# Search thresholds one and two of the second attention computed on GpSimd, the third prepared there, and a normalization ordered behind them

## Chip, cores and metric

The kernel runs on one core of a Trainium2 chip. Its time is the device time of one launch in microseconds (us); the median of three runs is given. A core has a matrix engine (TensorE, PE in the profile, with weight loads shown apart as PEld), a vector engine (VectorE, DVE), an engine for activation functions (ScalarE, ACT), a fourth one for elementwise work (GpSimd, POOL) and a queue that issues DMAs (SP). Each runs its own instructions in order, and they wait for each other through semaphores.

## What is computed

A graph network of four layers over 3327 nodes with 256 features, each followed by a residual and a layer norm. Only the fourth layer is touched. It runs two steps of a "top-p" attention beside a plain diffusion with the adjacency matrix:

```python
def _top_p_attention(X, W1, W2, W3):
    q = X @ W1.T @ W2.T
    k = X @ W3.T
    logits = q @ k.T / TAU
    probs = jax.nn.softmax(logits, axis=-1)
    idx = jnp.argsort(-probs, axis=-1)
    sp = jnp.take_along_axis(probs, idx, axis=-1)
    cs = jnp.cumsum(sp, axis=-1)
    keep_sorted = cs - sp < TOP_P
    rows = jnp.arange(probs.shape[0])[:, None]
    mask = jnp.zeros(probs.shape, dtype=bool).at[rows, idx].set(keep_sorted)
    A = probs * mask
    return A / jnp.maximum(A.sum(-1, keepdims=True), 1e-12)
...
for n in range(STEPS):
    A = _top_p_attention(Xa, W1, W2, W3)
    Xf = R @ Xf
    Xa = A @ Xa
    Z = Z + Xf @ U1[n].T + Xa @ U2[n].T
h = X + Z
mu = h.mean(-1, keepdims=True)
var = jnp.mean((h - mu) ** 2, axis=-1, keepdims=True)
return (h - mu) / jnp.sqrt(var + LN_EPS) * ln_g + ln_b
```

TOP_P is 0.9 and STEPS is 2; the result is added to the layer's input and normalized once more. So each row of 3327 probabilities keeps its largest entries until they hold 0.9 of the mass. Nothing is sorted in the kernel: it looks for the smallest value that is kept, row by row.

## The kernel before

The nodes are padded to 3328 and cut into 26 tiles of 128 rows. The second attention is a pipeline over these tiles, with three tiles in flight (the loop at line 1423). For one tile these pieces run:

- `scores` (line 1032): TensorE multiplies queries and keys, ScalarE copies the logits from PSUM into the tile `e` (128 x 3328), in four pieces.
- `search_long` (line 1162): finds each row's cut, and is the function that changes. It is a generator; the loop calls it step by step between TensorE's pieces of work. Its passes over all of `e` run on ScalarE, each with a sum along the row: an exponential at half scale (line 1177, `root`), the exponential itself (1179, `total`), a Relu and a Sign against the first threshold `c1` (1192, 1194: mass and count above it), and the same against a second threshold `c2` (1224, 1226). Between the passes stand short runs of arithmetic on one number per row: `c1` from `root` and `total` (1182 to 1190), `c2` by a step from the first mass and count (1196 to 1212), and the bound `c3` by a secant through both (1228 to 1238). `c3` lies above the cut by a margin, so that the cut is among the largest entries below it: VectorE writes each half of `e` with everything above `c3` set to zero (1244), takes the eight largest of each 128 columns (1111), ranks the largest 48 (1122, 1124), finds the cut `v` by a running sum (1131 to 1134), drops surplus equal values (1274) and masks `e` (1282).
- `attended` (line 1088): TensorE transposes the masked `e` block by block (1095), ScalarE copies the transposed blocks into `wt` (copies of this stage are listed under line 1030, where the in-order copy is made), TensorE multiplies them with `G` (1099).
- `diffused` (line 1072): adjacency tiles are loaded by SP (`at`, 1064), TensorE multiplies them with `F` (1066), VectorE scales the sum into `xf` (1085); GpSimd prepares its addend `t` (1076, 1080), part of which SP reloads from memory (`s` from `sd`, 1079).
- `second` (line 1323): the result's rows: VectorE adds attention and diffusion (1326), statistics (88, 89); GpSimd takes the root of the variance (829, 830), normalizes (1334 to 1336), then statistics again, and ScalarE writes the normalized rows (1345), which waits for GpSimd's `nb` (1344).

The order on each engine is made by a scheduler from the program's order and priorities, except where it is fixed: `here(...)` keeps an instruction in program order (all of ScalarE's passes and copies of this stage are kept so, and TensorE's score matmuls), and `tc.issue_after(x)` lets instructions be issued only after `x`. Before the change `issue_after(bound[0].ins)` holds the `match_replace` at line 1274 behind the last instruction of `c2` (line 1212). A row whose cut turns out not to be resolved to a tolerance sends its tile through a slow repeat (`again`, line 1532) after the loop.

Of the kernel before, what the change touches and what calls it, by code (L numbers as in the profile page):

```python
# [9 lines left out]
F32 = mybir.dt.float32  # L10
# [3 lines left out]
ALU = mybir.AluOpType  # L14
# [4 lines left out]
P = 128  # L19
# [28 lines left out]
def gnn_kernel(ctx: ExitStack, tc: tile.TileContext, n: int, a: dict, out: bass.AP):  # L48
# [771 lines left out]
    with tc.tile_pool(name="l3", bufs=1) as pool, tc.tile_pool(name="l3d", bufs=1, space=DRAM) as dram:  # L820
# [184 lines left out]
        sd = dram.tile([nt, P, D], F32, name="sd")  # L1005
        u1, u2 = (load(pool, x) for x in ("U1", "U2"))
        g3, b3 = (load_row(pool, x) for x in ("ln3_g", "ln3_b"))
        factors = pool.tile([P, 4], F32, name="factors")
        for k, x in enumerate((-0.5, -1.0, 0.3, 1.5)):
            nc.vector.memset(factors[:, k:k + 1], x)  # L1010
        ones = pool.tile([P, 8 * max(RP0, RPT)], F32, name="ones")
        nc.vector.memset(ones, 1.0)
# [144 lines left out]
            yield  # L1157

        junks = [None]
        bound = [None]  # L1160

        def search_long(work, sm, e, total, v, kept, halves=False):

# [4 lines left out]
            def t(name):  # L1168
                return t1(sm, name)
# [6 lines left out]
            yield  # L1176
            here(nc.scalar.activation(junk, e, AF.Exp, bias=neg[:, 0:1], scale=0.5, accum_out=root))
            yield
            here(nc.scalar.activation(e, e, AF.Exp, bias=neg[:, 1:2], accum_out=total))
            yield  # L1180
            lim = t("lim")
            nc.gpsimd.tensor_scalar(lim, total, -TOP_P, None, op0=ALU.mult)
            c1 = t("c1")
            nc.vector.reciprocal(c1, root)
            nc.vector.tensor_mul(c1, c1, total)
            nc.vector.scalar_tensor_tensor(c1, c1, 0.301, c1, op0=ALU.mult, op1=ALU.mult)


            nc1, f1, sg, k1, m1 = t("nc1"), t("fs1"), t("sg"), t("k1"), t("m1")
            nc.vector.tensor_scalar_mul(nc1, c1, -1.0)  # L1190
            yield
            here(nc.scalar.activation(junk, e, AF.Relu, bias=nc1, accum_out=f1))
            yield
            here(nc.scalar.activation(junk, e, AF.Sign, bias=c1, scale=-1.0, accum_out=sg))
            yield
            nc.vector.tensor_scalar(k1, sg, -0.5, npad / 2, op0=ALU.mult, op1=ALU.add)
            nc.vector.scalar_tensor_tensor(m1, k1, c1, f1, op0=ALU.mult, op1=ALU.add)
            rc, na = t("rc"), t("na")
            nc.vector.reciprocal(rc, c1)
            nc.vector.tensor_scalar(na, m1, lim, rc, op0=ALU.add, op1=ALU.mult)  # L1200

            den, nu, p, q = t("den"), t("nu"), t("p"), t("q")
            nc.vector.tensor_scalar(den, k1, 0.5, UNDER, op0=ALU.mult, op1=ALU.add)
            nc.vector.reciprocal(den, den)
            nc.vector.tensor_scalar(nu, na, UNDER, den, op0=ALU.add, op1=ALU.mult)
            nc.vector.tensor_scalar(p, nu, 0.0, 1.0, op0=ALU.max, op1=ALU.add)
            nc.vector.tensor_sub(q, p, nu)
            nc.vector.reciprocal(q, q)
            c2 = t("c2")
            nc.vector.scalar_tensor_tensor(c2, p, c1, q, op0=ALU.mult, op1=ALU.mult)  # L1210
            nc2, f2, k2, m2 = t("nc2"), t("fs2"), t("k2"), t("m2")
            bound[0] = nc.vector.tensor_scalar_mul(nc2, c2, -1.0)

            big = t("big")
            nc.gpsimd.tensor_tensor(big, k1, na, op=ALU.subtract)
            nc.gpsimd.tensor_scalar(big, big, 32.0, HUGE, op0=ALU.is_lt, op1=ALU.mult)

            s, dm, ends, same = t("s"), t("dm"), t1(sm, "ends", 2), t("same")
            nc.gpsimd.tensor_tensor(s, c2, c1, op=ALU.subtract)
            nc.gpsimd.tensor_scalar(same, s, 0.0, None, op0=ALU.is_equal)  # L1220
            nc.gpsimd.tensor_tensor(s, s, same, op=ALU.add)
            nc.gpsimd.tensor_scalar(ends, factors[:, 2:], k1, 1.0, op0=ALU.mult, op1=ALU.max)
            yield
            here(nc.scalar.activation(junk, e, AF.Relu, bias=nc2, accum_out=f2))
            yield
            here(nc.scalar.activation(junk, e, AF.Sign, bias=c2, scale=-1.0, accum_out=sg))
            yield
            nc.vector.tensor_scalar(k2, sg, -0.5, npad / 2, op0=ALU.mult, op1=ALU.add)
            nc.vector.scalar_tensor_tensor(m2, k2, c2, f2, op0=ALU.mult, op1=ALU.add)
            nc.vector.reciprocal(s, s)  # L1230
            nc.vector.tensor_sub(dm, m1, m2)
            nc.vector.tensor_mul(s, s, dm)
            nc.vector.tensor_scalar(s, s, ends[:, 0:1], ends[:, 1:2], op0=ALU.max, op1=ALU.min)
            nc.vector.reciprocal(s, s)
            c3 = t("c3")
            nc.vector.scalar_tensor_tensor(c3, c2, UNDER, m2, op0=ALU.mult, op1=ALU.add)
            nc.vector.tensor_scalar(c3, c3, lim, s, op0=ALU.add, op1=ALU.mult)
            nc.vector.scalar_tensor_tensor(c3, c3, c2, big, op0=ALU.add, op1=ALU.max)
            rest, base = t("rest"), t("base")
            cand = candidates(work)  # L1240
            for h, r in enumerate((rest, base)):
# [28 lines left out]
            for i, c in enumerate((0, half)):  # L1270
                drop = drops[:, i, :]
                part = e[:, c:c + half]
                with tc.issue_after(bound[0].ins):
                    nc.vector.match_replace(part[:, ::-1], drop, part[:, ::-1], 0.0)
                if halves:
                    nc.vector.scalar_tensor_tensor(part, part, v, part, op0=ALU.is_ge, op1=ALU.mult,
                                                   accum_out=sums[:, i:i + 1])
# [45 lines left out]
        def second(work, psum, it, acc, f, xf):  # L1323

            h = work.tile([P, D], F32, name="h")
            nc.vector.scalar_tensor_tensor(h, acc, f, xf, op0=ALU.mult, op1=ALU.add)
            xb = work.tile([P, D], F32, name="t")
            nc.gpsimd.tensor_tensor(xb, X[:, it, :], b3, op=ALU.add)
            mv = small.tile([P, 2], F32, name="mv")
            stats(mv, h)  # L1330
            rs = small.tile([P, 1], F32, name="rs")
            power(rs, mv)
            yield
            nc.gpsimd.tensor_scalar(h, h, mv[:, 0:1], rs, op0=ALU.subtract, op1=ALU.mult)
            nc.gpsimd.tensor_tensor(h, h, g3, op=ALU.mult)
            nc.gpsimd.tensor_tensor(h, h, xb, op=ALU.add)
            yield
            mv = small.tile([P, 2], F32, name="mv")
            stats(mv, h, here)
            rs = small.tile([P, 1], F32, name="rs")  # L1340
            power(rs, mv)
            yield
            nb = small.tile([P, 1], F32, name="nb")
            nc.gpsimd.tensor_scalar(nb, mv[:, 0:1], rs, -1.0, op0=ALU.mult, op1=ALU.mult)
            here(nc.scalar.activation(h, h, AF.Identity, scale=rs, bias=nb))  # L1345
            m = min(P, n - it * P)
            nc.sync.dma_start(out[it * P:it * P + m, :], h[:m, :])
            yield
# [29 lines left out]
        with tc.tile_pool(name="l3w", bufs=2) as work, tc.tile_pool(name="l3s", bufs=4) as sm, \  # L1378
# [41 lines left out]
            with tc.tile_pool(name="l3q", bufs=3, space=PSUM) as psum:  # L1420
                es, searches, xfs = {}, {}, []
                result = iter(())
                for i in range(-2, nt + 1):
# [52 lines left out]
                    if 0 < i:  # L1476
                        f = normalizer(sm, kepts[1][:, i - 1:i], tots[1][:, i - 1:i])
                        result = second(work, psum, i - 1, next(values), f, xfs[i - 1])
                both(result)
                fl = unresolved(sm, psum, 1)  # L1480

            fi0 = pool.tile([1, nt + 1], I32, name="fi0")
# [140 lines left out]
```

## Time and profile before

| | |
|---|---|
| median of three runs | 3515.73 us (3509.28, 3515.73, 3515.77) |
| the profiled execution: its time | 3512.67 us |
| the profiled execution: its span | 3510.8 us |
| granted TensorE clock over the span | 0.965 |
| busy PE | 3228.0 us (92%) |
| busy DVE | 2374.3 us (68%) |
| busy ACT | 1737.1 us (49%) |
| busy POOL | 932.2 us (27%) |
| first and last mask of the second attention (line 1282) start at | 2710.3 and 3449.0 us |

The shares are means over four layers with different limits; what a change in the second attention is worth has to be read in the stretch from about 2650 us to the end. There the stretches from one tile's first transpose to the next show how full each engine is, and the idle time ahead of TensorE's transposes shows who is late. Times in the rows are microseconds from the span's start; a bracket at the end of a row is the idle time of the engine ahead of it and what ended it. In rows of groups the first figure behind the bar is the sum of busy time in us, the second the mean of one instruction in ns.

### The profile page before, as it was taken

The page shows a single profiled execution, that of the slowest core. Times are in us where ns is not written, and L with a number is a line of the kernel's source. Part 1 is how long each engine was busy: PE and PEld are TensorE (multiplying, and loading weights), DVE is VectorE, ACT ScalarE, POOL GpSimd, SP SyncE. Part 2 cuts the span into 40 slices and gives each one's busy share as a digit, 9 for nine tenths or more (in the row PEclk, how much of TensorE's full clock was granted, in tenths as well). Part 3 has the DMA queues.
Part 4 walks back from the last instruction along what each step waited for, and adds up shares of the span by engine and source line. Part 5 has one row for each costly group of instructions (what it writes and reads, how often), then busy time and mean ns, then how long its engine had stood idle before and what let it go on. Part 6 is the DMA issues. An engine that isn't in the chain of part 4 may idle for free. (4 is left out here: it accounts for less than half of the span.)

```text
span 3510.8 us, 42847 instructions
## 1 busy us (share of the span) xinstructions
PE 3228.0 (92%) x15415; PEld 2526.5 (72%) x15415; DVE 2374.3 (68%) x5256; ACT 1737.1 (49%) x2749; POOL 932.2 (27%) x942
## 2 busy tenths in 40 slices
PE   9999888988988776999899999999997999999996
PEld 5888766666676555888677878777785777777775
DVE  2111168999999997777444444545434999999996
ACT  1000456767767674111233333333336888888883
POOL 0000055656665653111100000000001233333332
PEclk9999999999999888999899999999999999999998
DMA  5443334433443222444221212121212122222220
GB/s 179 147 151 122 112 104 115 113 106 118 101 115 90 67 58 92 131 142 149 84 67 49 65 48 67 50 64 53 61 48 73 55 57 69 66 69 61 70 66 16
DMA packets 138323, 304.62 MB, mean 87 GB/s; under 512 B 19086, under 2 KB 58574, under 8 KB 137966
## 3 DMA queue, kind: packets, MB, share of 16 engines
q1 hardware_dynamic: 138094, 301.72, 29.0%
q8 instruction: 125, 2.05, 0.2%
q14 instruction: 104, 0.85, 0.1%
HBM read 291.01 MB, written 10.65 MB: 86 GB/s over the span
## 5 line engine op out<-in xcount | busy, mean ns | idle before, releaser
L282 POOL TENSOR_TENSOR h<-du,row 128x2048 f32<-128x2048 f32 (+1 forms) x110 | 465.6, 4233 | 344.5 <-DVE hc L282 252.1
L282 DVE TENSOR_TENSOR_SCAN h<-dA,carry,h 128x512 f32<-128x512 f32 (+1 forms) x384 | 449.0, 1221 | 18.6 <-ACT dA L289 18.5
L289 ACT ACTIVATE dA<-t,A_log 128x512 f32<-128x512 f32 (+1 forms) x448 | 292.5, 658 | 146.3 <-DVE h L282 144.8
L1099 PE MATMUL acc<-X,wt 128*128 128x256 f32 x1352 | 346.3, 393 | 10.6 <-ACT wt L1097 10.2
L1066 PE MATMUL acc<-F,at 128*128 128x256 f32 x1352 | 354.3, 387 | 0.9 <-ACT q L840 0.6
L1099 PE MATMUL acc<-G,wt 128*128 128x256 f32 x1352 | 336.9, 392 | 5.5 <-ACT wt L1030 5.1
L1099 PEld LDWEIGHTS acc<-X,wt 128*128 128x128 f32 x1352 | 244.6, 191 | 106.2 <-issue 41.3
L1066 PE MATMUL acc<-X,at 128*128 128x256 f32 x1352 | 308.4, 381 | 0.0
L975 PE MATMUL acc<-F,at 128*128 128x257 f32 x1352 | 304.9, 382 | 1.3 <-DMA U<-in_U 1.3
L341 PE MATMUL cb<-F,at 128*128 128x256 f32 x1196 | 294.1, 394 | 4.8 <-ACT hn L361 3.4
L1099 PEld LDWEIGHTS acc<-G,wt 128*128 128x128 f32 x1352 | 250.7, 193 | 65.8 <-ACT wt L1030 35.2
L1111 DVE MAX8 cand<-e 128x8 f32<-128x128 f32 x676 | 142.2, 279 | 229.6 <-ACT e L1052 218.0
L118 PE MATMUL acc<-xa,at 128*128 128x257 f32 x1352 | 294.7, 380 | 0.0
L1066 PEld LDWEIGHTS acc<-F,at 128*128 128x128 f32 x1352 | 238.2, 191 | 75.3 <-issue 50.2
L118 PEld LDWEIGHTS acc<-xa,at 128*128 128x128 f32 x1352 | 255.9, 189 | 38.3 <-issue 0.5
L1066 PEld LDWEIGHTS acc<-X,at 128*128 128x128 f32 x1352 | 252.9, 191 | 40.3 <-issue 8.3
L975 PEld LDWEIGHTS acc<-F,at 128*128 128x128 f32 x1352 | 254.5, 191 | 37.3 <-issue 1.5
L632 PE MATMUL y<-ident,hc 128*128 128x128 f32 x1664 | 236.9, 297 | 46.2 <-DVE hc L282 46.1
L632 PEld LDWEIGHTS y<-ident,hc 128*128 128x128 f32 x1664 | 210.3, 154 | 87.5 <-DVE hc L282 62.8
L341 PEld LDWEIGHTS cb<-F,at 128*128 128x128 f32 x1196 | 229.4, 198 | 54.4 <-issue 14.5
L282 DVE TENSOR_TENSOR hc<-h,row 128x2048 f32<-128x2048 f32 (+2 forms) x114 | 242.3, 2127 | 11.0 <-PE y L632 4.3
L1097 ACT COPY wt<-tp 128x512 f32<-128x512 f32 (+1 forms) x182 | 93.6, 557 | 312.1 <-PE tp L1095 311.9
(351 smaller groups left out, 5219.4 us busy)
## 6 DMA issues: line engine op xcount, KB each, us to landing
at<-in_adjT SPq DMA_DIRECT2D x104, 832.0 KB, 4.5
at<-in_adjT SPq DMA_DIRECT2D x260, 320.0 KB, 3.0
row<-bc SPq DMA_DIRECT2D x80, 512.0 KB, 5.0
at<-in_adjT SPq DMA_DIRECT2D x52, 576.0 KB, 4.1
at<-in_adjT SPq DMA_DIRECT2D x26, 512.0 KB, 3.6
row<-bc SPq DMA_DIRECT2D x32, 384.0 KB, 4.8
qd<-q SPq DMA_DIRECT2D x104, 32.0 KB, 1.9
q<-qd SPq DMA_DIRECT2D x52, 64.0 KB, 1.9
```

Of the source, the lines that this page charges most:

```text
L118: nc.tensor.matmul(acc, at[:, j, :], rhs[:, j0 + j, :], start=(j0 + j == 0), stop=(j0 + j == nt - 1))
L282: return lambda *x, **k: tc.keep_in_program_order(op(*x, **k))
L289: decays.append(op(*x, **k))
L341: ten.matmul(acc, at[:, j % JC, :], X0[:, j, :], start=(j == 0), stop=(j == nt - 1))
L632: x = ten.matmul(y[:, g * P:(g + 1) * P], h[:, g, i * P:(i + 1) * P], ident, is_transpose=True, start=(first and g == 0), stop=(last and g ...
L975: nc.tensor.matmul(acc, at[:, j, :], F[:, j0 + j, :], start=(j0 + j == 0), stop=(j0 + j == nt - 1))
L1066: nc.tensor.matmul(acc, at[:, j, :], rhs[:, j0 + j, :], start=(j0 + j == 0), stop=(j0 + j == nt - 1))
L1097: copy(wt[:, :m, :], pt[:, :m, :])
L1099: nc.tensor.matmul(acc, wt[:, j, :], rhs[:, j0 + j, :], start=(j0 + j == 0), stop=(j0 + j == nt - 1))
L1111: nc.vector.max(cand[:, s * 8:(s + 1) * 8], z[:, s * SEG:(s + 1) * SEG])
```

## The change

The arithmetic of `c1` and `c2` is rewritten in a form that needs fewer steps and moved from VectorE to GpSimd. `root` is raised to the power -2 and multiplied by (0.301, -0.301) while ScalarE runs the second exponential; one instruction with `total` twice then gives `c1` and its negative side by side (`c1s`). The step to `c2` avoids one division by multiplying both its sides with the divisor; reciprocals are powers of -1; `c2` and its negative come from one instruction again. Sums that the bound needs (`s`, `double`, `high`, `ends`, `big`, `level`) are prepared on GpSimd, issued after `c2`; those with the second pass's Relu mass (`level`) wait for ScalarE. VectorE keeps eight instructions for `c3`, where ten stood, and none for `c1` and `c2`, where sixteen stood. The `match_replace` is no longer held behind `c2`. In `second`, the root of the variance and the first step of the normalization are issued after the instruction `lim` of the search that is latest at that point (`edge`); at the end of the loop `edge` is cleared.

```diff
-        factors = pool.tile([P, 4], F32, name="factors")
-        for k, x in enumerate((-0.5, -1.0, 0.3, 1.5)):
+        factors = pool.tile([P, 8], F32, name="factors")
+        for k, x in enumerate((-0.5, -1.0, 0.6, 3.0, 0.301, -0.301, -2.0, -1.0)):
...
+            squares = t1(sm, "squares", 2)
+            nc.gpsimd.tensor_tensor(root, root, factors[:, 6:7], op=ALU.pow)
+            nc.gpsimd.tensor_scalar(squares, factors[:, 4:6], root, None, op0=ALU.mult)
             here(nc.scalar.activation(e, e, AF.Exp, bias=neg[:, 1:2], accum_out=total))
             yield
-            lim = t("lim")
-            nc.gpsimd.tensor_scalar(lim, total, -TOP_P, None, op0=ALU.mult)
-            c1 = t("c1")
-            nc.vector.reciprocal(c1, root)
-            nc.vector.tensor_mul(c1, c1, total)
-            nc.vector.scalar_tensor_tensor(c1, c1, 0.301, c1, op0=ALU.mult, op1=ALU.mult)
...
-            nc.vector.tensor_scalar_mul(nc1, c1, -1.0)
+            def scaled(dst, x, a, b, op0, op1, engine=nc.gpsimd):
+                return engine.tensor_scalar(dst, x, a, b, op0=op0, op1=op1)
+
+            def inverse(dst, x):
+                nc.gpsimd.tensor_tensor(dst, x, factors[:, 7:8], op=ALU.pow)
+
+            c1s, lim, rc = t1(sm, "c1", 2), t("lim"), t("rc")
+            scaled(c1s, squares, total, total, ALU.mult, ALU.mult)
+            c1, nc1 = c1s[:, 0:1], c1s[:, 1:2]
+            edge[0] = nc.gpsimd.tensor_scalar(lim, total, -TOP_P, None, op0=ALU.mult)
+            inverse(rc, c1)
...
-            nc.vector.tensor_scalar(k1, sg, -0.5, npad / 2, op0=ALU.mult, op1=ALU.add)
-            nc.vector.scalar_tensor_tensor(m1, k1, c1, f1, op0=ALU.mult, op1=ALU.add)
-            nc.vector.reciprocal(rc, c1)
-            nc.vector.tensor_scalar(na, m1, lim, rc, op0=ALU.add, op1=ALU.mult)
-            nc.vector.tensor_scalar(den, k1, 0.5, UNDER, op0=ALU.mult, op1=ALU.add)
-            nc.vector.reciprocal(den, den)
-            nc.vector.tensor_scalar(nu, na, UNDER, den, op0=ALU.add, op1=ALU.mult)
-            nc.vector.tensor_scalar(p, nu, 0.0, 1.0, op0=ALU.max, op1=ALU.add)
-            nc.vector.tensor_sub(q, p, nu)
-            nc.vector.reciprocal(q, q)
-            nc.vector.scalar_tensor_tensor(c2, p, c1, q, op0=ALU.mult, op1=ALU.mult)
-            bound[0] = nc.vector.tensor_scalar_mul(nc2, c2, -1.0)
+            scaled(k1, sg, -0.5, npad / 2, ALU.mult, ALU.add)
+            scaled(m1, k1, c1, f1, ALU.mult, ALU.add)
+            scaled(room, k1, 0.5, UNDER, ALU.mult, ALU.add)
+            scaled(na, m1, lim, rc, ALU.add, ALU.mult)
+            scaled(more, na, UNDER, 0.0, ALU.add, ALU.max)
+            nc.gpsimd.tensor_tensor(more, more, room, op=ALU.add)
+            scaled(less, more, na, UNDER, ALU.subtract, ALU.subtract)
+            inverse(less, less)
+            second_cut = scaled(c2s, c1s, more, less, ALU.mult, ALU.mult)
+            c2, nc2 = c2s[:, 0:1], c2s[:, 1:2]
...
+            with tc.issue_after(second_cut.ins):
+                scaled(s, c1, c2, 1e-30, ALU.subtract, ALU.add)
+                scaled(double, m1, lim, 2.0, ALU.add, ALU.mult)
+                scaled(high, c2, 2.0 * UNDER, double, ALU.mult, ALU.add)
+                scaled(ends, factors[:, 2:4], k1, 2.0, ALU.mult, ALU.max)
+                nc.gpsimd.tensor_tensor(big, k1, na, op=ALU.subtract)
+                scaled(big, big, 32.0, HUGE, ALU.is_lt, ALU.mult)
+                scaled(level, f2, m1, 2.0, ALU.subtract, ALU.mult)
+                scaled(level, c2, float(npad), level, ALU.mult, ALU.add)
             here(nc.scalar.activation(junk, e, AF.Sign, bias=c2, scale=-1.0, accum_out=sg))
             yield
-            nc.vector.tensor_scalar(k2, sg, -0.5, npad / 2, op0=ALU.mult, op1=ALU.add)
-            nc.vector.scalar_tensor_tensor(m2, k2, c2, f2, op0=ALU.mult, op1=ALU.add)
             nc.vector.reciprocal(s, s)
-            nc.vector.tensor_sub(dm, m1, m2)
-            nc.vector.tensor_mul(s, s, dm)
-            nc.vector.tensor_scalar(s, s, ends[:, 0:1], ends[:, 1:2], op0=ALU.max, op1=ALU.min)
+            scaled(x, sg, nc2, level, ALU.mult, ALU.add, nc.vector)
+            scaled(s, x, s, ends[:, 0:1], ALU.mult, ALU.max, nc.vector)
+            nc.vector.tensor_add(c3, x, high)
+            nc.vector.tensor_scalar(s, s, ends[:, 1:2], None, op0=ALU.min)
             nc.vector.reciprocal(s, s)
-            nc.vector.scalar_tensor_tensor(c3, c2, UNDER, m2, op0=ALU.mult, op1=ALU.add)
-            nc.vector.tensor_scalar(c3, c3, lim, s, op0=ALU.add, op1=ALU.mult)
-            nc.vector.scalar_tensor_tensor(c3, c3, c2, big, op0=ALU.add, op1=ALU.max)
+            scaled(c3, c3, s, c2, ALU.mult, ALU.add, nc.vector)
+            nc.vector.tensor_scalar(c3, c3, big, None, op0=ALU.max)
...
-                with tc.issue_after(bound[0].ins):
-                    nc.vector.match_replace(part[:, ::-1], drop, part[:, ::-1], 0.0)
+                nc.vector.match_replace(part[:, ::-1], drop, part[:, ::-1], 0.0)
...
             rs = small.tile([P, 1], F32, name="rs")
-            power(rs, mv)
             yield
-            nc.gpsimd.tensor_scalar(h, h, mv[:, 0:1], rs, op0=ALU.subtract, op1=ALU.mult)
+            with tc.issue_after(edge[0].ins) if edge[0] else nullcontext():
+                power(rs, mv)
+                nc.gpsimd.tensor_scalar(h, h, mv[:, 0:1], rs, op0=ALU.subtract, op1=ALU.mult)
...
                 both(result)
+                edge[0] = None
```

In the order of instructions that this gives in the middle of the loop, GpSimd has 37 instructions per tile where it had 22, and VectorE's sixteen and two are gone. ScalarE's order is the same. On TensorE the first transposes of the first four tiles stand a few diffusion matmuls earlier; the rest of its order in the loop is the same. On SP the reload of `s` (1079) stands behind one more adjacency load per tile. On VectorE the reciprocal of `s` (line 1231 of the changed file) stands among the ranking of the previous tile or directly behind it, and waits there for GpSimd; the first instruction on the Sign's count waits for ScalarE and for GpSimd's `level`. On GpSimd the second power for `root` (1180) and `level` follow `c2`, then the addend `t` of line 1327, `neg`, `c1s`, `lim`, and only then the normalization of the previous tile's result.

## Prediction

> **What bounds the kernel now.** The change lies in the second attention only, so I read that stretch. First the windows, one per tile, from one first transpose to the next; columns: length, then busy time and instructions of PE, PEld, DVE, ACT, POOL, then clock and DMA:
>
> ```profile
> 2805.81:2836.37 30.56, 28.44 (x138) 21.48 (x139) 29.41 (x100) 25.72 (x26) 11.04 (x22) 1.00 0.20 57
> 2930.54:2961.13 30.59, 30.40 (x147) 22.64 (x147) 29.33 (x97) 25.86 (x26) 10.86 (x22) 1.00 0.23 67
> 3052.13:3083.11 30.98, 30.41 (x147) 22.56 (x147) 29.69 (x100) 25.97 (x26) 11.15 (x22) 1.00 0.22 66
> ```
>
> TensorE and VectorE are both nearly full: 30.4 us of matmuls in a normal tile (28.4 in four early ones, which hold 44 diffusion matmuls instead of 52) beside 29.4 to 29.7 us of VectorE work that, with the gaps between its instructions, fills the tile. Who is late is seen in TensorE's timeline:
>
> ```profile
> 2714.03 1.97 PE L1095 MATMUL tp<-ident,e 128*128 128x128 f32 x8 [14.34 <-DVE e L1282]
> 2836.37 1.07 PE L1095 MATMUL tp<-ident,e 128*128 128x128 f32 x8 [2.00 <-DVE e L1282]
> 2961.13 1.99 PE L1099 MATMUL acc<-G,wt 128*128 128x256 f32 x8 [0.19 <-ACT wt L1030]
> 3083.11 0.63 PE L1095 MATMUL tp<-ident,e 128*128 128x128 f32 x4 [0.57 <-DVE e L1282]
> 3452.87 1.79 PE L1095 MATMUL tp<-ident,e 128*128 128x128 f32 x12 [3.25 <-DVE e L1282]
> ```
>
> TensorE waits for VectorE's mask: 14.34 us once, while the pipeline fills; 2.00, 1.42, 2.00 and 2.26 in four early tiles (7.7); 0.36 and then 12 times about 0.56 from 3021 on (7.1); 1.66 at 3423.66 and 3.25 at 3452.87. Nothing else holds it but copies of `wt`, 0.19 in three tiles. If VectorE were free, only these sums could be won; a VectorE saving beyond them is hidden by 30.4 us of matmuls.
>
> **What leaves VectorE.** The groups give means:
>
> ```profile
> L1185 DVE TENSOR_TENSOR c<-c,tot 128x1 f32<-128x1 f32 x26 | 16.5, 633 | 2.5 <-ACT e L1179 2.5
> L1222 POOL TENSOR_SCALAR ends<-factors,k 128x2 f32<-128x2 f32 x26 | 9.0, 348 | 125.6 <-DVE k L1196 125.6
> L1251 POOL TENSOR_SCALAR base<-base,rest,tot 128x1 f32<-128x1 f32 x26 | 10.0, 384 | 57.1 <-DVE z L1244 57.1
> L1216 POOL TENSOR_SCALAR big<-big 128x1 f32<-128x1 f32 x26 | 6.3, 242 | 2.4
> L830 POOL TENSOR_TENSOR rs<-rs,mhalf 128x1 f32<-128x1 f32 x52 | 30.5, 587 | 4.3
> ```
>
> Sixteen instructions of `c1` and `c2` sum to 3.3 us a tile (L1185 0.63, the other fifteen 0.15 to 0.27). Ten for `c3` (1.88) become eight: four of the two-operand kind at 0.27 or less, four at 0.15, 1.6 together. That frees 3.6 us of 29.7, with some 0.4 of gaps.
>
> **What GpSimd takes.** Fifteen instructions more per tile, some 4.5 us at 0.3, to 15.7 of 30.4: not full. What counts is the chain from the Sign's count to `c2`, which ScalarE's next pass needs. Nine steps by the nearest rows: two with one pair of constants 0.24 each and `room` 0.24 (L1216), two with two per-row operands 0.38 each (L1251), a sum 0.19 (L1215), `less` 0.30 (L1252), a power 0.59 (L830), the pair `c2s` 0.40 (L1222, L1251): 2.96. Gaps between dependent steps are 0.08 to 0.1 (L829 to L830): 0.8. Chain 3.8 us; bounds 2.1 (nine of the cheapest row, 0.19, short gaps) and 6.1 (nine at 0.59). ScalarE's timeline says how much fits:
>
> ```profile
> 3005.51 3.07 ACT L1194 ACTIVATE junk<-e,c 128x3328 bf16<-128x3328 f32 x1
> 3013.83 0.58 ACT L1030 COPY wt<-tp 128x512 f32<-128x512 f32 x1 [0.76 <-PE tp L1095]
> 3014.32 3.07 ACT L1224 ACTIVATE junk<-e,nc 128x3328 bf16<-128x3328 f32 x1
> 3017.85 3.07 ACT L1226 ACTIVATE junk<-e,c 128x3328 bf16<-128x3328 f32 x1
> ```
>
> The count lands at 3008.67, `c2` would be there at 3012.5, the Relu starts at 3014.32: 1.8 us of cover. If it is gone, each us over it stops ScalarE, then `wt`, then TensorE. In the early tiles the distance from count to Relu is 3.9 to 4.5 us: cover almost none. `c1` costs one step (0.4) after `total` at 3025.47, and is needed at 3031.64.
>
> **VectorE's new tile.** Bound 1.75 and MAX8 of line 1172 0.5; two halves of z with MAX8 9.05; ranking to `drops` 7.6 (3004.03 to 3011.61); two replaces 3.8; mask 3.7; `xf`, `h`, statistics 1.7: 28.1 us, under 30.4. It will run ahead by some 2.3 us and wait for the last diffusion matmul (L1066 ends at 3020.81) at line 1085. The bound then starts 1.8 later, at 3022.6. So TensorE's waits for the mask go, and TensorE alone sets the tile.
>
> **Normalization moved.** Four big steps (L1334 1.25, L1335, L1336 0.73, `rs`) start after `lim`, about 3026.3 instead of 3022.85; behind them wait L1076, L1080, `base`, `nb`. They end near 3032.9, plus up to 2 us of collisions; VectorE's second statistics come at 3034, ScalarE's L1345 at 3039 with `nb` at 3037: hidden, and 2 us from mattering. The reload of `s` goes behind one more load on SP (0.33 issue, some 2 us to land), read a tile later: nothing. In the first four tiles the first transposes stand two to four diffusion matmuls earlier, under 0.9 us, where the mask is over 1 us early: nothing. Four more memsets, 0.06 each, at 1383: 0.24 at most.
>
> **The shared port.** One row speaks against moving work here:
>
> ```profile
> 2863.10 3.68 DVE L1282 SCALAR_TENSOR_TENSOR e<-e,v 128x3328 f32<-128x3328 f32 x1
> 2863.26 4.10 POOL L1328 TENSOR_TENSOR t<-X,ln_b 128x256 f32<-128x256 f32 x1 [3.51 <-DVE xf L1085]
> ```
>
> The same L1328 takes 0.73 elsewhere; it ended only when the mask did. L1335 takes 2.24 against 0.73 in the tail for the same reason (line 1244), and L1185's 0.69 against 0.16 is the reverse. So a two-tensor step of the chain (`more` sum, power) under a mask would add up to 3.7 us. In the middle of the loop the new mask ends 26.4 us after the bound's start, so it lies at 3014.9 to 3018.6 of this clock (one tile of 30.4 taken off), the chain at 3008.7 to 3012.5: 2.4 us apart.
>
> The rows also price one step on both engines: a pair of constants takes 0.24 on GpSimd (L1216), 0.15 on VectorE (L1203). The Trainium skill ("GPSIMD Engine Reference", section "Engine selection") speaks against the move: elementwise work belongs on VectorE, GpSimd being about 2x slower for two inputs. By that rule the chain would be an estimated 4.1 us, twice VectorE's 2.06 from L1196 to L1212, and the sum 0.3 us worse in the fill.
>
> **The fill gets worse.** ScalarE's first Relu against `c2` starts 0.55 late (chain 3.8 against a pass of 3.2 between). In tile 0's ranking VectorE now waits for tile 1's `s`: count at 2700.4 (2700.67 less the 0.8 that ScalarE waited for `c1` there, plus 0.55), chain with `t` (0.72) inside 4.5, then four steps, `s` at 2706.3; after it 0.15 + 0.38 + 2.5 until the replaces, 2709.4 against 2706.43: +3.0. Bounds: -1.2 (interleaved `c2` work gone, no wait) and +7.5 (chain 6.1 in both tiles).
>
> **The tail.** The last count lands at 3451.49, but L1228 starts at 3453.87 and z at 3455.97, since VectorE was in the previous mask until 3452.64. Free VectorE: z at 3453.3, -2.7; from there to the end the chain is unchanged. Bounds 0 and -2.7.
>
> **Sum against the profiled span.** Fill +3.0; early tiles -7.7; middle -4.7 (7.1 less 13 times 0.19 of `wt` waits that show in its place); 3423.66 -1.7; tail -2.7 (the 3.25 lies in it). -13.8: span 3497.0. The profiled execution took 3512.67, giving 3498.9; the median shown is 3 us above that, giving 3501.9. I take 3501.
>
> **Rivals.** (1) The gain is mostly used up: fill +7.5, early tiles half (cover gone there), rest as above: -5.5, 3510. For it: the thin early cover; against: the GpSimd rows repeat within a few ns. (2) Slower: the chain is caught under the mask because VectorE runs ahead. Place: power at `c2`; price 3.7 - 1.8 = 1.9 us in each of 22 tiles, 42, and 3.7 in the fill, on top of the -13.8: +32, 3548. From 7 caught tiles on it eats the gain, from 11 on the kernel is slower by over 0.2%. For it: VectorE's lead moves its mask towards the chain; against: 2.4 us of distance remain. (3) A row falls outside its bound because powers round differently: one tile of the repeat is 28 passes like L1282's 3.7, over 100 us: 3620 or more. Against: the formulas are the same, and the bound keeps a margin of 24 entries.
>
> **Chances.** Forecast 0.68, (1) 0.18, (2) 0.12, (3) 0.02. A change under 0.2% (7 us) can't be told from none. Faster 0.68, same 0.18, slower 0.14. Low: fill -1.2, all 7.1, `wt` waits gone (0.9), -21.3 from the median, and from the lowest run 3509.28: 3488. High: fill +7.5 and only the tail won: 3520.
>
> **What would show it.** Right: no `tp` wait on the mask after the fill; VectorE waiting for L1066 at line 1085; tiles at 30.4 to 30.6; a longer first wait, near 17; ScalarE's Relu not waiting for `c2` in the middle. Wrong: waits of ScalarE on `c2` each tile, or GpSimd powers of several us under the mask.

## The result and the profile after

| | before | after |
|---|---|---|
| median of 12 runs each | 3511.91 us (3509.22 to 3515.97) | 3508.72 us (3502.66 to 3512.03) |
| ratio of after to before | | 0.9989, 95% interval 0.9981 to 0.9997 |
| span of the profiled execution | 3510.8 us | 3506.1 us |
| busy DVE, POOL | 2374.3 us, 932.2 us | 2315.5 us, 1122.1 us |

The kernel is 3.2 us faster (0.1%; the interval goes from 0.03 to 0.19%) where 13.8 were forecast. The time lies inside the range of 3488 to 3520, but the likeliest case, 3501, did not come true.

To see where the gain stayed, I measure within the profiled executions from the first diffusion product of the second attention (line 1066) to the last product of line 1099. The layers ahead end up to 16 us apart from one profiled execution to the next, with the same code; this stretch leaves them out. Its lengths, here and below, come from one profiled execution of each kernel. It is cut at the ends of VectorE's masks (the 25 instructions of line 1281, or 1282 before); the eighth mask stands where the early tiles are over.

| stretch | before | after | difference | predicted |
|---|---|---|---|---|
| start to first mask (fill) | 65.31 | 67.28 | +1.97 | +3.0 |
| first to 8th mask (early tiles) | 214.15 | 208.85 | -5.30 | -7.7 |
| 8th to 24th mask (middle) | 495.39 | 489.40 | -5.99 | -6.4 |
| 24th mask to last product (tail) | 70.37 | 75.79 | +5.42 | -2.7 |
| sum | 845.22 | 841.32 | -3.90 | -13.8 |

(-6.4 is the middle and the wait of 3423.66, which ends with the 24th mask.) TensorE's timeline of the changed kernel shows the same; columns are start, duration, engine, line, operation and count, and in brackets the idle time ahead and what ended it:

```profile
2715.20 1.97 PE L1095 MATMUL tp<-ident,e 128*128 128x128 f32 x8 [16.90 <-DVE e L1281]
2741.35 1.06 PE L1095 MATMUL tp<-ident,e 128*128 128x128 f32 x8 [1.12 <-DVE e L1281]
2772.07 1.06 PE L1095 MATMUL tp<-ident,e 128*128 128x128 f32 x8 [2.45 <-DVE e L1281]
2804.35 1.06 PE L1095 MATMUL tp<-ident,e 128*128 128x128 f32 x8 [2.37 <-DVE s L1231]
2835.00 0.63 PE L1095 MATMUL tp<-ident,e 128*128 128x128 f32 x4 [2.33 <-DVE s L1231]
2929.22 1.99 PE L1099 MATMUL acc<-G,wt 128*128 128x256 f32 x8 [0.19 <-ACT wt L1030]
3446.31 2.79 PE L1095 MATMUL tp<-ident,e 128*128 128x128 f32 x12 [4.73 <-DVE e L1281]
```

The first wait grew to 16.90. The four early waits for the mask, which were to vanish, are 8.3 us together, where 7.7 stood. (Where the bracket names `s`, the mask had ended just ahead of that reciprocal.) From then on only 0.19 for a copy of `wt` is left in each tile, and the wait of 1.66 at 3423.66 is gone: the middle is as predicted. The wait for the last whole mask grew from 3.25 to 4.73.

The cut at VectorE's masks also counts how far VectorE runs ahead, and that changed: TensorE starts a tile's transposes 3.59 us after the 8th mask's end (0.77 before) and 2.50 after the 24th (0.15 before). So the same stretch, cut where TensorE starts the transposes of these tiles (at 2714.03, 2928.89 and 3423.66 before, at 2715.20, 2927.56 and 3415.88 after), shows better what TensorE gained:

| stretch, cut at the transposes | before | after | difference | predicted |
|---|---|---|---|---|
| fill | 65.37 | 67.35 | +1.98 | +3.0 |
| early tiles | 214.86 | 212.36 | -2.50 | -7.7 |
| middle | 494.77 | 488.32 | -6.45 | -6.4 |
| tail | 70.22 | 73.29 | +3.07 | -2.7 |

The middle came as forecast, and the fill cost 1 us less. The early tiles gave a third of their forecast, and the tail lost 3 us where it should have won.

One early and one middle tile by windows (length, then busy time and instructions of PE, PEld, DVE, ACT, POOL, then clock and DMA):

```profile
2804.35:2835.00 30.65, 28.32 (x138) 21.42 (x139) 27.47 (x82) 25.43 (x26) 18.51 (x36) 1.00 0.19 57
2929.22:2959.81 30.59, 30.40 (x147) 22.63 (x147) 27.25 (x82) 25.86 (x26) 18.89 (x37) 1.00 0.23 68
```

In the middle TensorE is busy for 30.40 of 30.59 us: nothing is left to win there. In the early tile VectorE does 1.9 us less than before (27.47 against 29.41), and the tile is as long as before; 28.32 of 30.65 are TensorE's. So something other than VectorE's load sets this tile.

VectorE's timeline shows where its freed time went:

```profile
2704.69 0.16 DVE L1231 RECIPROCAL s<-s 128x1 f32<-128x1 f32 x1 [2.77 <-POOL s L1185]
...
2744.18 0.48 DVE L1325 SCALAR_TENSOR_TENSOR h<-acc,f,xf 128x256 f32<-128x256 f32 x1 [1.55 <-PE acc L1099]
...
2926.23 0.48 DVE L1325 SCALAR_TENSOR_TENSOR h<-acc,f,xf 128x256 f32<-128x256 f32 x1 [1.46 <-PE acc L1099]
...
2928.04 0.27 DVE L1185 TENSOR_SCALAR x<-sg,c,level 128x1 f32<-128x1 f32 x1 [0.64 <-ACT junk L1228]
...
3435.74 0.16 DVE L1231 RECIPROCAL s<-s 128x1 f32<-128x1 f32 x1 [2.80 <-POOL s L1185]
```

At 2704.69, in the first tile's ranking, VectorE waits for the second tile's `s`, as predicted. At 3435.74 the same happens in the last ranking but one, which was not predicted. In the middle it waits at `h` and `x`, 2.1 us a tile.

### The profile page after: what moved, and what is told of

Its sections match the earlier page's. It is cut to its first block, busy times and chain, and to the rows that moved or that the text cites. A ratio compares the mean times of both kernels' runs of the same rounds, so it can differ in the third digit from the quotient of the medians.

```text
span 3506.1 us, 42765 instructions
## 1 busy us (share of the span) xinstructions
PE 3224.0 (92%) x15415; PEld 2524.5 (72%) x15415; DVE 2315.5 (66%) x4792; ACT 1736.4 (50%) x2749; POOL 1122.1 (32%) x1332
```

## The experiments

Each ratio is to runs of the kernel before on the same chip, and the lengths are those of the stretch above (before 845.2, after 841.3).

### One edit at a time

The reciprocal behind the bound's first instruction:

```diff
-            nc.vector.reciprocal(s, s)
-            scaled(x, sg, nc2, level, ALU.mult, ALU.add, nc.vector)
+            mass = scaled(x, sg, nc2, level, ALU.mult, ALU.add, nc.vector)
+            with tc.issue_after(mass.ins):
+                nc.vector.reciprocal(s, s)
```

> The reciprocal of s on VectorE is issued behind the bound's first instruction x, so that VectorE no longer waits for GpSimd's s inside the ranking of the tile before. Theory (the wait of 2.8 us for s costs the fill and the tail): the first wait of TensorE for the mask falls from 16.9 to about 14.1 us, and tile 24's ranking is no longer held for 2.8 us before the last masks, so its wait of 4.7 at 3446 falls to about 2; together 4 to 6 us less than the changed kernel, about 3503 on its scale of 3508.7. Rival (the longer fill comes from ScalarE waiting 1.5 us for c2, and VectorE's stop is spare time): the first wait stays over 16 and the time within 1 us.

Measured: ratio 0.9968 (0.9953 to 0.9982), 835.8 us: 5.5 under the changed kernel, as the theory said. Its TensorE timeline:

```profile
2706.09 1.97 PE L1095 MATMUL tp<-ident,e 128*128 128x128 f32 x8 [14.21 <-DVE e L1282]
...
3434.77 1.50 PE L1095 MATMUL tp<-ident,e 128*128 128x128 f32 x12 [2.04 <-DVE e L1282]
```

The fill is 64.61 (2.7 less), the tail 72.88 (2.9 less), the early tiles are unchanged (208.92). ScalarE still waits 0.40 and 1.25 for `c2` in the fill, so the rival is out: the fill's loss was VectorE's wait for `s` alone.

The sum `h` behind the first half of `z`:

```diff
+                else:
+                    lead[0] = x
...
-            nc.vector.scalar_tensor_tensor(h, acc, f, xf, op0=ALU.mult, op1=ALU.add)
+            with tc.issue_after(lead[0].ins) if lead[0] else nullcontext():
+                nc.vector.scalar_tensor_tensor(h, acc, f, xf, op0=ALU.mult, op1=ALU.add)
...
-                edge[0] = None
+                edge[0] = lead[0] = None
```

> The sum h of the tile before is issued on VectorE behind the first half of z, so that the bound doesn't stand behind it. Theory (a closed loop in the early tiles: mask, transposes, diffusion products, last products of the tile before, h, bound, next mask): the four early waits of TensorE for the mask (1.1, 2.5, 2.4, 2.3, together 8.3 us) fall under 2 in all, 5 to 7 us less than the changed kernel; VectorE's waits at h for the last products (45 us) nearly vanish. Rival (the early masks are late because the thresholds' chain on ScalarE and GpSimd is): the four waits stay within 2 us of 8.3 and x waits for ScalarE or GpSimd instead. Risk: the normalization starts some 3 us later, and the last row's chain in the tail grows by up to 2 us.

Measured: ratio 0.9982 (0.9972 to 0.9992), 841.7 us: nothing won. TensorE's early waits are 0.64, 2.46, 1.93 and 1.90, together 6.9. VectorE waits at `h` only at the end, but now waits at `x` for ScalarE's last pass (in total, times, longest; 16.0 us in 19 times in the changed kernel):

```profile
DVE x L1186 <- ACT junk L1229: 60.3, 21, 5.1
```

So my theory that the loop closes through `h` fell: `h` only filled a wait for ScalarE that is there anyway. The third tile even came 34.2 us after the second. GpSimd's and then ScalarE's timeline of this run show why:

```profile
2742.36 3.57 POOL L1186 TENSOR_SCALAR c<-c,more,less 128x2 f32<-128x2 f32 x1
```

```profile
2745.96 3.07 ACT L1216 ACTIVATE junk<-e,c 128x3328 bf16<-128x3328 f32 x1 [2.77 <-POOL c L1186]
```

The step that makes `c2`, 0.34 elsewhere, began just after VectorE's mask (2742.03 to 2745.72) and ended with it. ScalarE's pass waited 2.77. That is the prediction's slower rival, in one tile. It is near in the changed kernel too: there the same step starts at 2737.35 and takes 0.34, and the mask starts at 2737.51, 0.16 us behind the step instead of 0.33 ahead of it.

TensorE's order alone, as before the change:

```diff
-                for j in range(m):
-                    nc.tensor.transpose(pt[:, j, :], e[:, (j0 + j) * P:(j0 + j + 1) * P], ident)
+                with tc.issue_after(last[0].ins) if tp > 2 and last[0] and j0 == 0 else nullcontext():
+                    for j in range(m):
+                        nc.tensor.transpose(pt[:, j, :], e[:, (j0 + j) * P:(j0 + j + 1) * P], ident)
...
-                    nc.tensor.matmul(acc, wt[:, j, :], rhs[:, j0 + j, :],
-                                     start=(j0 + j == 0), stop=(j0 + j == nt - 1))
+                    mm = nc.tensor.matmul(acc, wt[:, j, :], rhs[:, j0 + j, :],
+                                          start=(j0 + j == 0), stop=(j0 + j == nt - 1))
+                if tp > 2:
+                    last[0] = mm
```

> Only TensorE's order is put back as in the kernel before: the first transposes of a tile are issued behind the last products of the tile before; VectorE, GpSimd and ScalarE keep the changed kernel's order. Theory (the transposes standing ahead of the products close the loop through h): the four early waits fall from 8.3 to under 2 us, 5 to 7 us less than the changed kernel. Rival (the order on TensorE does not matter, only VectorE's order or the length of the search): the waits stay at 6 or more and the time within 1.5 us.

Measured: ratio 0.9963 (0.9949 to 0.9977), 835.7 us, 5.6 less. No early wait for the mask is left. TensorE's timeline of the kernel before first (the third tile), then of the changed kernel (the second), then of this run (the third):

```profile
2770.57 1.13 PE L1099 MATMUL acc<-G,wt 128*128 128x256 f32 x4
2771.64 0.97 PE L1046 MATMUL sc<-kT,q 64*128 64x416 f32 x4
2774.61 2.73 PE L1095 MATMUL tp<-ident,e 128*128 128x128 f32 x12 [2.00 <-DVE e L1282]
```

```profile
2741.35 1.06 PE L1095 MATMUL tp<-ident,e 128*128 128x128 f32 x8 [1.12 <-DVE e L1281]
2742.25 1.03 PE L1066 MATMUL acc<-F,at 128*128 128x256 f32 x4
2743.12 1.03 PE L1099 MATMUL acc<-G,wt 128*128 128x256 f32 x4
2744.07 0.97 PE L1046 MATMUL sc<-kT,q 64*128 64x416 f32 x4
```

```profile
2771.47 1.89 PE L1066 MATMUL acc<-F,at 128*128 128x256 f32 x8
2773.20 1.03 PE L1100 MATMUL acc<-G,wt 128*128 128x256 f32 x4
2774.16 0.97 PE L1046 MATMUL sc<-kT,q 64*128 64x416 f32 x4
2775.06 1.53 PE L1096 MATMUL tp<-ident,e 128*128 128x128 f32 x12
```

In the kernel before, the transposes waited behind the last products of the tile before and four score matmuls. In the changed kernel the transposes, which need the mask, stand ahead of products and scores that don't. So the mask also holds back the last products of the tile before and the logits (`sc`) that ScalarE copies for a later search, and the mask after next comes late again. Put behind them, the transposes find the mask ready. The run before says through what: not through `h`, which waits for the products, but through ScalarE, for whose last pass VectorE waits. That it is the logits, and not the copies of `wt`, that ScalarE lacks, isn't separated. Of the 5.6 us, 4.35 went from the early tiles; the other 1.25 lie in the tail, behind the 25th mask, and are the clock's, told below. The second tile's mask caught the step of `c2` here too (3.75 us, ScalarE waited 2.95).

The normalization's move undone:

```diff
-            with tc.issue_after(edge[0].ins) if edge[0] else nullcontext():
+            with nullcontext():
                 power(rs, mv)
```

> The normalization is not held behind lim; its GpSimd steps and the addend t stand ahead of neg, c1 and lim of the next searches again, everything else as in the changed kernel. Theory (the move only orders GpSimd's queue and neither costs nor gains in the early tiles): neg and c1 come up to 5 us later, so ScalarE waits for them in the middle; the time is between 0 and 10 us above the changed kernel. Rival (the move is where the missing gain went, through t and base standing behind the normalization): the time falls by 3 us or more.

Measured: ratio 0.9989 (0.9978 to 1.0001), 841.1 us: no difference in the sum. But the early tiles are 1.2 us longer (210.03 against 208.85; 1.0 cut at the transposes), and a shorter tail makes up for it, whose last matmuls run at a granted clock of 1.00 instead of 0.90. So the move gains about 1 us, and it is not where the missing gain went.

### Both edits together, and a guard

> Both edits that helped, together: the reciprocal of s behind x, and the first transposes behind the last products of the tile before. From the start of the stage to the last product the two runs before took 835.8 and 835.7 us against 841.3 in the changed kernel. Theory (two separate losses, the wait for s in the fill and the tail, and the closed loop through TensorE's order in the early tiles): they add up, 830 to 831 us, some 15 us under the kernel before. Rival (one loss seen from two sides, for each edit frees the same VectorE time): 834 to 836, no better than either alone.

Measured: ratio 0.9941 (0.9926 to 0.9956), median 3492.06 against 3510.12 us; the stretch takes 827.8 us, better than the sum of the two, for the most part because here the second tile's mask caught a step behind `c2` and ScalarE didn't wait: the distance to the next mask is 30.03 us, where it was 33.82 with TensorE's order alone. That is luck: the mask started 0.30 us after the step, where it had started 0.15 ahead of it. This version beats both kernels. TensorE's waits in it (in total, times, longest), then one early tile by windows:

```profile
PE tp L1096 <- DVE e L1286: 16.3, 2, 14.2
PE acc L1100 <- ACT wt L1030: 8.7, 24, 3.8
PE tp L1096 <- DVE e L1280: 5.6, 1, 5.6
```

```profile
2769.35:2797.98 28.63, 28.40 (x140) 21.45 (x138) 27.18 (x81) 25.35 (x26) 17.82 (x35) 1.00 0.23 67
```

An early tile now takes 28.63 us, of which TensorE works 28.40; it took 30.65. The mask is waited for in the fill and the tail only.

| stretch, cut at the masks | after | reciprocal | TensorE's order | both |
|---|---|---|---|---|
| fill | 67.28 | 64.61 | 67.27 | 64.61 |
| early tiles | 208.85 | 208.92 | 204.50 | 199.93 |
| middle | 489.40 | 489.43 | 489.40 | 489.44 |
| tail | 75.79 | 72.88 | 74.53 | 73.77 |

The guard makes the mask wait for the next tile's `c2`:

```diff
+            cut[0] = c2
...
+                done = nc.vector.match_replace(part[:, ::-1], drop, part[:, ::-1], 0.0)
...
+                with tc.issue_after(done.ins):
+                    seen = nc.vector.tensor_copy(t("seen"), cut[0])
+                with tc.issue_after(seen.ins):
                     nc.vector.scalar_tensor_tensor(e, e, v, e, op0=ALU.is_ge, op1=ALU.mult, accum_out=kept)
```

> The same two edits, and the mask on VectorE is issued behind a one-wide copy of the next tile's c2, so that no mask can catch the chain to c2 on GpSimd. Theory (a mask that catches the step c2s costs ScalarE 3 us in the second tile, as 2.95 us in the run with the transposes behind the products, and nowhere else): ScalarE's wait for c2 there falls under 0.5 us, and the time is 0 to 3 us below the run without the guard; the copies (25 times 0.15) lie in VectorE's spare time. Rival (the mask waits for c2 in tiles where it needn't): 1 to 5 us above it.

Measured: ratio 0.9947 (0.9932 to 0.9963), 827.0 us, no difference: there was nothing to guard any more. Up to the 24th mask it is 1.2 us longer (the second tile's wait), and its shorter tail is the clock's, told below.

### How near the chain is to the mask

The middle of the changed kernel on GpSimd, then on VectorE:

```profile
2918.78 0.34 POOL L1185 TENSOR_SCALAR c<-c,more,less 128x2 f32<-128x2 f32 x1
...
2919.89 0.30 POOL L1185 TENSOR_SCALAR s<-c,c 128x1 f32<-128x1 f32 x1
2920.30 3.72 POOL L1185 TENSOR_SCALAR high<-c,double 128x1 f32<-128x1 f32 x1
```

```profile
2920.23 0.16 DVE L1231 RECIPROCAL s<-s 128x1 f32<-128x1 f32 x1 [0.19 <-POOL s L1185]
2920.31 3.67 DVE L1281 SCALAR_TENSOR_TENSOR e<-e,v 128x3328 f32<-128x3328 f32 x1
```

Each middle mask catches a step of the chain, `high`, but `c2` was done 1.2 us earlier. The reciprocal, which waits for `s`, holds the mask back until then, though only by 0.15 us: in the first experiment, without it, `c2` is done 1.04 us ahead of the mask. Two runs with five idle steps in the chain ask what that is worth:

```diff
             inverse(less, less)
+            for _ in range(5):
+                scaled(less, less, 1.0, 0.0, ALU.mult, ALU.add)
             second_cut = scaled(c2s, c1s, more, less, ALU.mult, ALU.mult)
```

> The reciprocal behind x, as in the first experiment, and five one-wide multiplications by 1 added on GpSimd between the power and c2s in each tile (some 1.5 us). In the middle c2s stands 1.2 us ahead of the mask in the changed kernel, so it now starts under the mask. The prediction's rival (a chain caught under the mask costs each tile up to the mask's 3.7 us less the cover): c2s takes 3.6 us, c2 comes 2.8 us after the Relu could start, in some 22 tiles; with nothing to absorb it 22 x 2.8 = 60 us, so 20 to 60 us above the first experiment. Against it (ScalarE is idle for 4 us in each tile and absorbs the wait): under 5 us above.

Measured: ratio 1.0151 (1.0132 to 1.0171), 895.2 us, 59 above the first experiment. ScalarE's waits in the whole stage:

```profile
ACT junk L1217 <- POOL c L1185: 51.2, 23, 4.2
```

From the ninth mask on, every mask of the middle catches a step of the chain: `c2s` itself in four tiles, one of the five idle steps in the other twelve. One of them on GpSimd, and the mask on VectorE:

```profile
3048.88 3.59 POOL L1185 TENSOR_SCALAR c<-c,more,less 128x2 f32<-128x2 f32 x1
```

```profile
3048.57 3.69 DVE L1284 SCALAR_TENSOR_TENSOR e<-e,v 128x3328 f32<-128x3328 f32 x1
```

Each of these tiles is 2.5 to 3.7 us longer than 30.59. ScalarE's idle time doesn't absorb it: TensorE's waits for ScalarE's copies `wt` sum to 42.4 us, where they were 9.4 in the first experiment.

> The same five steps in the changed kernel itself, where the reciprocal of s stands ahead of the mask. Theory (the reciprocal's wait is a brake: VectorE's mask waits for s, which is computed behind c2, so the mask can't catch c2): c2s stays at 0.34 us, VectorE waits some 1.7 us for s in each tile of the middle, and ScalarE's Relu still finds c2 (cover 2.1 us); the time is 0 to 10 us above the changed kernel, through the fill (2 x 1.5) and the tail (1.5) above all. Rival (the reciprocal doesn't protect): as the run without it, 20 to 60 us above.

Measured: ratio 1.0027 (1.0016 to 1.0039), 851.0 us, 9.7 above the changed kernel. Cut at the transposes, that is 2.3 in the fill, 1.2 in the tail, and 6.1 in the early tiles, which I had not priced. The middle stays at 30.59 a tile: VectorE waits at the reciprocal and the mask starts after `c2`:

```profile
3051.09 0.16 DVE L1233 RECIPROCAL s<-s 128x1 f32<-128x1 f32 x1 [1.57 <-POOL s L1185]
3051.17 3.67 DVE L1283 SCALAR_TENSOR_TENSOR e<-e,v 128x3328 f32<-128x3328 f32 x1
```

With the same five steps the two runs differ in what stands ahead of the mask. So the reciprocal that costs the fill and the tail 2.7 to 2.9 us each is also a brake that keeps the mask off `c2`. At the second tile's mask, where the reciprocal stands behind the mask, the five steps took 4.61 us and ScalarE waited 4.23.

### How much of VectorE's saving is used

Steps of 128x16 on `drops` were added to the version with both edits:

```diff
+            for _ in range(8):
+                nc.vector.tensor_scalar(drops, drops, 1.0, 0.0, op0=ALU.mult, op1=ALU.add)
```

> The kernel with both edits, and eight multiplications of drops by 1 added on VectorE ahead of the replaces in each tile (128x16, some 0.17 us each: 1.4 us a tile, 36 us of work in all). Theory (in the middle the change freed more VectorE time than TensorE can use: VectorE waits 1.46 us for the last products at h and 0.64 for ScalarE at x in each tile): the middle stays at 30.59 us a tile, and only the fill and the tail grow, by 1.4 each: 2 to 4 us above the run with both edits, 3494 to 3496. Rival (VectorE is still as binding as before): 1.4 us in most tiles, 25 to 36 us above.

Measured: ratio 0.9978 (0.9965 to 0.9991), 838.0 us, 10.3 more than without. The middle stays at 30.59 a tile. But the early tiles grew by 9.1 us (6.2 cut at the transposes; the rest is VectorE's lead, which is gone), where I had expected nothing: seven times 1.4 is 9.8, so they have little spare VectorE time. ScalarE waited 2.54 for one `c2` there. No mask caught that one; in GpSimd's order the addend `t` stands inside the chain, and it waited for VectorE, where the added steps stand:

```profile
2790.18 0.73 POOL L1334 TENSOR_TENSOR t<-X,ln_b 128x256 f32<-128x256 f32 x1 [2.85 <-DVE drop L1275]
```

With 20 such steps:

> Twenty such steps, some 3.5 us a tile: as much VectorE time as the change took away (3.6 us). Theory (spare time of 2.1 us in the middle): 1.4 us a tile are over; they show as waits of TensorE for the mask in some 24 tiles, 25 to 40 us above the run with both edits, and with the fill and the tail 30 to 45. Rival (the spare time is larger, for the mask could come later without TensorE's noticing): under 10 us above, through fill and tail alone.

Measured: ratio 1.0127 (1.0112 to 1.0143), 891.7 us, 64 more. The middle tile takes 32.29 us, 1.7 more, near the 1.4 expected; the early tiles pay nearly the whole load (23.8 us in seven; 20.2 cut at the transposes), which I had left out. TensorE's waits for the mask are back: 63.4 us, 25 times, the fill's 18.6 among them.

The version with both edits, with the edit that undoes the normalization's move:

> The kernel with both edits, without the normalization held behind lim. Theory (the order of GpSimd's queue there is hidden as long as neg and c1 come in time, as in the run without the move alone, 0 to 2 us above): 0 to 2 us above the run with both edits. Rival (with the early waits gone the late neg and c1 show): 3 to 10 us above.

Measured: ratio 0.9955 (0.9941 to 0.9969), 827.8 us, the same to 0.1 us, but by chance: the early tiles are 1.2 us longer (0.8 cut at the transposes), as in the run without the move alone, and the tail is 0.95 shorter. The move is worth about 1 us, far less than either edit.

The kernel before with its replaces no longer held behind `c2`, and nothing else:

```diff
-                with tc.issue_after(bound[0].ins):
-                    nc.vector.match_replace(part[:, ::-1], drop, part[:, ::-1], 0.0)
+                nc.vector.match_replace(part[:, ::-1], drop, part[:, ::-1], 0.0)
```

> The kernel before, with one part of the change alone: the replaces are no longer held behind c2, which stays on VectorE. The scheduler then puts replaces and mask (7.5 us) ahead of the steps of c2. Theory (c2 is due at ScalarE some 4 us after the count lands): c2 comes 4 to 7 us later, ScalarE waits 2 to 4 us in each of 24 tiles: 40 to 90 us above the kernel before; so the release pays only because c2 has left VectorE. Rival (the release is the part that helps): 0 to 10 us below the kernel before.

Measured: ratio 1.0417 (1.0401 to 1.0433), 995.3 us, 150 more than before, where 40 to 90 were expected. ScalarE's timeline, one middle tile (37.6 us long):

```profile
3002.85 3.07 ACT L1224 ACTIVATE junk<-e,nc 128x3328 bf16<-128x3328 f32 x1 [7.76 <-DVE nc L1212]
```

With `c2` on VectorE its last steps stand behind replaces and mask, and ScalarE waits 7.4 us a tile (178.0 in 24). So the release alone costs. What it gains in the changed kernel no run shows: none has `c2` on GpSimd and the replaces held behind it.

## Why the prediction was right or wrong

- **VectorE's saving.** Its busy time fell by 2.4 us a middle tile (29.69 to 27.25), not 3.6: durations of neighbouring short instructions overlap in the rows (`x` at 2928.04 lasts 0.27; the next two start at 2928.35 and 2928.54, and the first of these lasts 0.28), so their sum is more than the time they take. With the gaps that leaves the 2.1 us of waits seen, near the predicted 2.3; but they lie at `h` (line 1325) and `x`, not at line 1085.
- **GpSimd's chain.** 3.44 us (2915.68 to 2919.12) against 3.8 predicted, cover 2.1 us against 1.8. The prediction's estimate of 4.1 by the Trainium skill ("GPSIMD Engine Reference", "Engine selection") doubled the time of eleven steps on VectorE, and GpSimd has nine. From step to step it is 0.38 us on GpSimd against 0.19 on VectorE before, so the page's factor of about 2 agrees with this chain; the count was wrong.
- **Fill.** Right in mechanism: with VectorE's wait for `s` undone it took 64.61, less than before (65.31). The size was +1.97 instead of +3.0.
- **Middle and the wait at 3423.66.** Right: -6.45 cut at the transposes (-5.99 at the masks) against -6.4, with the 0.19 of `wt` in each tile.
- **Early tiles.** -2.50 cut at the transposes, for -7.7. The step that failed is the sentence that gave the earlier transposes "nothing". I looked at whether the mask comes in time for the transposes, from the timeline of before, and not at what stands behind them on TensorE if it doesn't. The move was also longer than the "two to four diffusion matmuls, under 0.9 us" that it was taken for: in the rows of 2742.25 to 2744.97 the transposes stand ahead of four diffusion matmuls, four products and four scores, 2.7 us. The waits stayed (8.3 us); with the order undone they went, and cut at the transposes the early tiles took 208.02, 6.84 less than before, near the forecast 7.7, though a mask caught `c2` there.
- **Tail.** The larger miss: +3.07 cut at the transposes (+5.42 at the masks) for -2.7. "Free VectorE: z at 3453.3" took VectorE as free, but on the way there, from 3415 to 3436, it waits for `h` 1.46, for `x` 0.65 and for `s` 2.80. The first two only use up VectorE's lead, of which 2.50 were left at the 24th mask; the third is lost. I had priced the wait for `s` in the fill and not looked for it in the last ranking but one. Undoing it gave 2.9 back; from the 25th mask on another 1.85 were lost (43.01 against 41.16), most of it to the clock. About 1 us of the 5.8 stays open.
- **Rivals.** The time is that of rival 1, but not for its reasons: its fill of +7.5 didn't come and the cover held. Rival 2's mechanism was nearer than my 2.4 us of distance: 1.2 in the middle with the reciprocal holding the mask, 1.0 without it. Its price, 1.9 a tile, was met by 2.5 to 3.7, but in a run whose chain is five steps longer and has that much less cover. No repeat of a tile (rival 3) appeared.
- **The sum.** Of the 9.9 us that are missing between -13.8 and -3.9, the tail has 5.8 and the early tiles 5.2; the fill gives 1.0 back. That the time still lies in the range is owed to a range wide enough for both misses.

## What to carry to other kernels

Before an order change on an in-order engine is priced at nothing, name what stands behind the moved instruction: if the moved one waits, they all wait, and a loop over engines can close. An engine freed by moving work elsewhere keeps that time only if none of its remaining instructions waits for the moved work; look for the first reader of each moved result in every stage, the last tiles included. A margin between a short chain and a long instruction that blocks it should be measured before either is made faster.

## What the runs showed of the hardware

- A GpSimd step of one number per row that starts under VectorE's mask (which reads `e` twice) ends only when the mask does, even if it reads only one-wide operands: `high` 3.72 us against 0.29 elsewhere, `c2s` 3.57 against 0.34. The prediction had this only for steps with two tensors. Under the replaces and MAX8, which read one, the chain ran at its usual 0.19 to 0.57. The Trainium skill ("SBUF — State Buffer", "Who interferes with whom") says so: a VectorE instruction with two inputs contends with any GpSimd instruction that reads SBUF. These runs agree.
- The granted clock at the end is not the same in all runs. The last of three windows from the 25th mask's end, in the kernel before, in the changed kernel and in the guarded one (the clock is the third figure from the end):

```profile
3478.72:3493.88 15.16, 14.94 (x80) 12.50 (x79) 4.47 (x18) 4.10 (x8) 4.55 (x8) 1.00 0.03 10
```

```profile
3472.16:3489.17 17.01, 16.59 (x80) 13.83 (x80) 4.82 (x20) 4.19 (x8) 4.57 (x8) 0.90 0.03 9
```

```profile
3452.38:3467.66 15.28, 15.06 (x80) 12.63 (x80) 4.56 (x18) 4.09 (x8) 4.57 (x8) 1.00 0.03 10
```

The same 80 matmuls take 16.59 us at 0.90 and 15.06 at 1.00. In the 13 us ahead of them, in which TensorE partly waits, the clock was 0.74, 0.87 and 0.74: the lower clock falls into the wait or into the products. In the kernel with both edits it was 0.93 ahead and 0.85 in the products, and the window took 17.50 us. So about 2 us of a tail's length can be the clock's. What decides where it falls was not tried.
